# Seventy short unread products in a small planned stage: filling TensorE's waits in the first layer of a four-layer network

## The chip, the cores and the metric

The kernel runs on one core of a Trainium2 chip. The metric is the device time of one execution in microseconds (us), the median of a few executions; smaller is better. Beside the timed executions there is one profiled execution, whose span runs from its first to its last instruction.

A NeuronCore has five engines that work side by side and wait for each other on semaphores: TensorE (PE in the profile, its weight loads PEld), VectorE (DVE), ScalarE (ACT), GpSimd (POOL) and SyncE (SP), which only issues transfers here. Each engine takes its own instructions strictly in the order of its list. TensorE writes into PSUM, of which the kernel uses eight banks of 128 x 512 floats.

## The reference, cut to what matters

Four sub-layers follow each other on an input of 8 x 256 tokens with 128 features; after each comes a residual and a layer norm. The change lies in the first two.

```python
x = L0_attn_x                                       # 8 x 256 x 128
# first: a linear attention with a per-batch summary
Q = l2norm(x @ W_q.T); K = l2norm(x @ W_k.T); V = x @ W_v.T
x = layernorm(x + Q * (sum over tokens of K * V) / 128)
# second: a router and eight experts, two of them per token
h = layernorm(x @ Wr1 + br1) * ln_scale + ln_bias
logits = gelu(h) @ Wr2 + br2
p = softmax(logits); take the two largest, normalise them
x = layernorm(x + sum over the two experts of share * expert(x))
...
# then a convolution with four linear attentions, and a gated network
```

## The kernel before, in words

The 2048 tokens are worked as four blocks (`blk` 0 to 3) of 512 tokens, each block as four tiles of 128.

**The opening (lines 417 to 588).** `first_layer(blk)` describes one block's path through attention and router as a list of steps, each with an engine, a cost in ns, what it reads and writes, and the PSUM bank it needs. The steps of one block that matter below, by their names and lines:

- `project` (L440): four products per block, copied out by ACT (L443).
- `sums` (L475): four products that sum K * V over the tokens. They need `rk`, a reciprocal root from POOL (L334, L335), and `kv` from DVE (L467). `attend` (DVE, L486) reads the result, `residual` (L495) and `moments` (L343, L345) follow.
- `turned_s` (L503): four transposes; ACT copies them out (L509).
- `router` (L515): four products of 64 columns into the bank `pr`; `scaled` (DVE, L540) and another `moments` read them.
- `turned` (L559): two transposes of the normed router features `hn` (DVE, L550), then the gelu on ACT (L565).
- `choices` (L571): two products of 16 columns into `pl`, and DVE adds the bias into `logits` (L576).

`top_two` (L389 to L397) are thirteen DVE steps that pick two experts per token, once for blocks 0 and 1 and once for blocks 2 and 3. Their last step (L397) writes `taken`.

All these steps go into one object, `opening = Steps(...)` (L417). `Steps.order` is a list scheduler: it simulates the engines with the written costs, takes at each point the engine that can start first, and among the steps that this engine could start within `look` (50 ns) of that moment the one of highest rank plus bias. `Steps.trace` then emits the instructions in that order, under a manual schedule. So the costs in the code are used only to fix the order of each engine's list; on the chip an instruction starts when its data are there and its predecessor is out of the way.

**The counting stage (lines 595 to 689)** follows with a hand-written order. A DVE scan makes `upto` out of `taken` (L598). Two TensorE products (L603, L604) into the bank `pc` turn it into counts per expert. DVE works out of `pc` (L616 to L674) which slot each token gets; POOL finds the `owners` (L631 to L637), the expert of each of 23 work tiles. DVE then makes one-hot rows (L678) in four parts and TensorE multiplies 32 of them (L682), from which the list `source` comes.

In this stage TensorE also runs products that nobody reads: `busy(p)` multiplies the identity with 512 columns of a table (L593). Six stand behind L604 and four behind L682.

**Then the experts (lines 709 to 833):** SP loads an expert's weights per work tile as soon as `owners` is known, POOL gathers the rows by `source` (L749), and TensorE works in the order `turn` (L758), `widen` (L769), `narrow` (L782). The rest of the network, from line 835 on, has its own `Steps` object with its own list.

Of the kernel before, what the change touches and what calls it, by code (L numbers as in the profile page):

```python
# [220 lines left out]
def tile_network(ctx: ExitStack, tc: tile.TileContext, a: dict, out: bass.AP):  # L221
    nc = tc.nc
# [26 lines left out]
    def ps():  # L249
        return psp.tile([P, TB], F32, tag="ps", name="ps")  # L250
# [10 lines left out]
    ident = const.tile([P, P], F32, tag="ident", name="ident")  # L261
# [9 lines left out]
    def soon(shape, src, tag, pool=once):  # L271
        t = pool.tile(shape, F32, tag=tag, name=tag)
        nc.scalar.dma_start(out=t, in_=src)
        return t

    wqkv = soon([P, 3 * D], a["wqkv"], "wqkv")
# [42 lines left out]
    def tab(name):  # L319
        return tabs[:, TABS[name][0] : TABS[name][1]]  # L320
# [53 lines left out]
    def top_two(at):  # L374


        n = at.stop - at.start
        wide = [P, n, E]
        rev = mark("rev").unsqueeze(1).to_broadcast(wide)

        def spread(v):
            return v[:, at].unsqueeze(2).to_broadcast(wide)

        given, less, eq = logits[:, at, :], rest[:, at, :], key[:, at, :]
        steps = []
        for k, src in enumerate((given, less)):
            one = tops[:, k, at, :]
            steps += [
                lambda k=k, src=src: nc.vector.tensor_reduce(best[k][:, at], src, AX.X, ALU.max),  # L389
                lambda k=k, src=src: nc.vector.tensor_tensor(eq, src, spread(best[k]), ALU.is_equal),  # L390
                lambda: nc.vector.tensor_mul(eq, eq, rev),
                lambda: nc.vector.tensor_reduce(km[:, at], eq, AX.X, ALU.max),
                lambda one=one: nc.vector.tensor_tensor(one, eq, spread(km), ALU.is_equal),
            ]
            if k == 0:
                steps.append(lambda one=one: nc.vector.scalar_tensor_tensor(less, one, -1e30, given, ALU.mult, ALU.add))
        steps.append(lambda: nc.vector.tensor_add(  # L397
            taken[:, :, at].rearrange("p e i -> p i e"), tops[:, 0, at, :], tops[:, 1, at, :]))
        return steps
# [14 lines left out]
    nc.scalar.activation(once.tile([P, 1], F32, tag="warm", name="warm"), ones[:, 0:1], AF.Gelu_apprx_tanh)  # L414


    opening = Steps({"ps": [ps() for _ in range(8)]}, 50)  # L417

    def first_layer(blk):
        xT, x, w = xTs[blk], xs[blk], {}  # L420
# [3 lines left out]
        def do(engine, cost, run, reads="", writes="", later=0, new=""):  # L424
            def of(names):
                return [f"{n}.{blk}" for n in names.split()]

            opening.add(
                engine, cost, run, of(reads), of(writes) + of(new), {name: "ps" for name in of(new)}, bias=(0, -2464, -8107, -5328)[blk] - later
            )  # L430
# [127 lines left out]
                at = slice(i * P, (i + 1) * P)  # L558
                nc.tensor.transpose(T("pT")[:, at], w["hn"][:, at], ident)  # L559

        do("PE", 450, turned, "hn", new="pT")

        def gelu():
            w["hT"] = tmp()[:, : NT // 2 * P]
# [7 lines left out]
                    T("pl")[:, i * E : (i + 2) * E], lhsT=w["hT"][:, i // 2 * P : (i // 2 + 1) * P], rhs=wr2, start=True, stop=True  # L572
                )

        do("PE", 700, choices, "hT", new="pl")
        do("DVE", 190, lambda: nc.vector.tensor_add(  # L576
            logits[:, blk * NT : (blk + 1) * NT, :], T("pl")[:, : NT * E].rearrange("p (i e) -> p i e", i=NT), biases[:, R:].unsqueeze(1).to_broadcast([P, NT, E])
        ), "pl", "logits")

    for blk in range(NB):  # L580
        first_layer(blk)
    for blocks in ((0, 1), (2, 3)):
        for i, run in enumerate(top_two(slice(blocks[0] * NT, (blocks[-1] + 1) * NT))):
            opening.add(
                "DVE", 165 + 40 * len(blocks), run, [f"logits.{blk}" for blk in blocks] if i == 0 else [f"tops.{blocks[0]}"],
                [f"tops.{blocks[0]}"], bias=0 if blocks[-1] == NB - 1 else -50000,
            )
# [3 lines left out]
    def busy(p):  # L591

        return nc.tensor.matmul(p, lhsT=ident, rhs=tab("cos"), start=True, stop=True)  # L593


    with tc.manual_schedule():
# [2 lines left out]
            upto.rearrange("p e i -> p (e i)"), mark("later"), taken.rearrange("p e i -> p (e i)"), 0.0, ALU.mult, ALU.add  # L599
        )  # L600
        per_lane = upto[:, :, NTT - 1]
        pc = ps()
        nc.tensor.matmul(pc[:, 0:E], lhsT=ones, rhs=per_lane, start=True, stop=True)  # L603
        nc.tensor.matmul(pc[:, E : 2 * E], lhsT=mark("before"), rhs=per_lane, start=True, stop=True)  # L604

        idle = ps()
        for _ in range(6):
            busy(idle)

# [771 lines left out]
```

## Time and profile before

| what | us |
|---|---|
| median of 3 timed executions | 551.79 (551.04 to 553.66) |
| profiled execution, its own time | 549.38 |
| its span | 547.5 |
| opening, up to the last `logits` (L576) | ends at 42.97 |
| counting, up to the first gather (L749) | 42.97 to 59.15 |
| first TensorE instruction of the experts (L758) | 63.16 |
| the same stage's second `widen` (L769) | 69.55 |

TensorE is busy 508.9 us of the span (93%), DVE 283.9, ACT 221.0, POOL 212.1. These shares belong to the whole; the change touches only the first 59 us, where TensorE is not always the busiest.

How to read the views that come below. In the page's slices a digit is the busy share of one fortieth of the span, 13.7 us, in tenths, and `PEclk` is the clock that TensorE was granted, in tenths of full speed. A timeline row has the start, the length, the engine, the line, the operation, the tiles, the shape and the number of instructions merged into it, then in brackets the idle time before it and what ended it. A float32 product appears as two MATMUL rows, since it is done in two passes: the six `busy` of L593 are counted as twelve. A transpose is one pass. The chain of waits lists start, length, engine and line of the work that decided the end.

### The profile page before, as it was taken

To read this page: it belongs to the slowest core of one execution; us is meant where nothing else is said; L and a number is where in the kernel's file an instruction comes from. 1 tells how busy PE (TensorE), PEld (TensorE's weight loads), DVE (VectorE), ACT (ScalarE), POOL (GpSimd) and SP (SyncE) were. 2 spreads that over 40 slices of the span, in tenths; PEclk is the share of its full clock that TensorE was granted. 3 is DMA by queue.
4 is the path that set the end of the run, shared out by engine and by line. 5 is a ranking of instruction groups with operands and counts; after the bars stand their busy time and mean duration, and the time that the engine had idled before them with its cause. 6 is when DMAs were issued, how large, how long until landed. Compare 5 with 4: busy or idle time off the path is not lost.

```text
span 547.5 us, 7855 instructions
## 1 busy us (share of the span) xinstructions
PE 508.9 (93%) x2657; PEld 336.9 (62%) x2657; DVE 283.9 (52%) x955; ACT 221.0 (40%) x516; POOL 212.1 (39%) x310
## 2 busy tenths in 40 slices
PE   5877689999999999999999999989999999999992
PEld 3663478978999654458787886744444444444442
DVE  2887323433444385379899898687505530021212
ACT  3861223433444134237686868544224211322210
POOL 1971565666644321137666767361301000000001
PEclk9955989999999999999999999999999999999997
DMA  7951666665572320000000000000000000000010
GB/s 240 348 193 47 202 209 181 223 224 184 175 273 93 102 80 1 1 0 2 1 2 1 1 2 2 0 1 0 1 1 0 0 19 1 0 0 0 2 38 19
DMA packets 22889, 39.29 MB, mean 72 GB/s; under 512 B 3041, under 2 KB 16097, under 8 KB 22721
## 3 DMA queue, kind: packets, MB, share of 16 engines
q1 hardware_dynamic: 19088, 33.14, 18.4%
q0 software_dynamic: 2496, 5.12, 3.4%
q10 hardware_dynamic: 1264, 0.54, 0.4%
q8 instruction: 21, 0.34, 0.3%
q14 instruction: 20, 0.16, 0.1%
HBM read 34.13 MB, written 4.65 MB: 71 GB/s over the span
## 4 chain that ended last, share of the span: by engine, by line
PE 66%; DVE 12%; POOL 8%; issue 6%; DMA 4%; ACT 2%; SPq 1%; another core or an unknown queue 0%; POOLq 0%; DVEq 0%; ACTq 0%
PE ps L1256 20%; PE ps L769 10%; PE ps L1236 5%; PE ps L782 4%; POOL root L335 3%; PE ps L1277 3%; PE ps L997 2%; POOL ys L793 2%; PE ps L1017 2%; PE ps L1162 2%; DVE stats L878 2%; PE ps L1203 2%; PE ps L923 2%; PE ps L1192 2%; PE ps L1127 2%
## 5 line engine op out<-in xcount | busy, mean ns | idle before, releaser
L334 POOL TENSOR_SCALAR root<-mv 128x4 f32<-128x4 f32 (+1 forms) x46 | 12.5, 272 | 208.3 <-DVE mv L880 206.5
L769 PE MATMUL ps<-xT,hid 128*128 128x256 f32 (+1 forms) x368 | 75.2, 355 | 6.3 <-issue 5.9
L769 PEld LDWEIGHTS ps<-xT,hid 128*128 128x128 f32 x368 | 61.3, 194 | 15.3 <-issue 8.4
L775 DVE SCALAR_TENSOR_TENSOR gate<-ps,hid,gl 128x256 f32<-128x256 f32 (+1 forms) x92 | 38.6, 441 | 59.3 <-ACT gl L774 29.7
L774 ACT ACTIVATE gl<-ps,hid 128x256 f32<-128x256 f32 (+1 forms) x92 | 38.3, 445 | 50.4 <-PE ps L769 32.7
L1256 PE MATMUL ps<-t,gh 128*128 128x512 f32 x128 | 58.4, 592 | 0.0
L1256 PE MATMUL ps<-hid,gh 128*128 128x512 f32 x128 | 58.2, 592 | 0.0
L335 POOL TENSOR_TENSOR root<-root,minus_half 128x4 f32<-128x4 f32 (+1 forms) x54 | 55.1, 1020 | 4.5
L749 POOL DMA_INDIRECT xg<-x,source x39 | 37.8, 968 | 33.3 <-PE ps L769 11.0
L793 POOL DMA_INDIRECT ys<-y,dest x39 | 38.4, 984 | 23.6 <-DVE y L788 13.8
L1256 PEld LDWEIGHTS ps<-hid,gh 128*128 128x128 f32 x128 | 24.2, 190 | 29.7 <-issue 28.9
L1256 PEld LDWEIGHTS ps<-t,gh 128*128 128x128 f32 x128 | 24.0, 190 | 28.7 <-issue 28.7
L782 PE MATMUL ps<-hid,gate 128*128 128x128 f32 x312 | 38.8, 276 | 0.8 <-DVE gate L775 0.8
L782 PEld LDWEIGHTS ps<-hid,gate 128*128 128x128 f32 x312 | 37.9, 192 | 1.8 <-DVE gate L775 1.0
L1241 DVE SCALAR_TENSOR_TENSOR t<-t,ps 128x512 f32<-128x512 f32 x16 | 10.9, 681 | 51.2 <-ACT t L1239 51.2
L912 ACT ACTIVATE t<-t,shift,root 128x128 f32<-128x128 f32 x64 | 26.4, 482 | 10.8 <-POOL shift L892 10.8
L1236 PE MATMUL ps<-featT,g 128*128 128x512 f32 x64 | 30.2, 592 | 0.0
L1239 ACT ACTIVATE t<-ps,half 128x512 f32<-128x512 f32 x16 | 11.0, 687 | 41.3 <-PE ps L1236 41.3
L1113 POOL TENSOR_TENSOR t<-t,t 128x512 f32<-128x512 f32 x16 | 20.4, 1272 | 17.3 <-DVE t L1101 17.3
L1261 ACT ACTIVATE t<-ps,cols 128x512 f32<-128x512 f32 x16 | 11.0, 687 | 36.3 <-PE ps L1256 36.2
L923 PEld LDWEIGHTS ps<-ident,t 128*128 128x128 f32 x144 | 17.2, 141 | 11.6 <-issue 7.5
L878 DVE BATCH_NORM_STATS2 stats<-ps 128x6 f32<-128x128 f32 x48 | 10.7, 285 | 22.2 <-PE ps L923 22.1
(197 smaller groups left out, 940.9 us busy)
## 6 DMA issues: line engine op xcount, KB each, us to landing
hid<-in_experts_dram SPq DMA_DIRECT2D x23, 836.0 KB
got<-ys SPq DMA_DIRECT2D x6, 256.0 KB
counts<-in_counts_dram SPq DMA_DIRECT2D x1, 1032.0 KB
featT<-in_xT_dram SPq DMA_DIRECT2D x4, 256.0 KB
res<-in_x_dram SPq DMA_DIRECT2D x4, 256.0 KB
gh<-in_h1T_dram SPq DMA_DIRECT2D x1, 1024.0 KB
gh<-in_h2T_dram SPq DMA_DIRECT2D x1, 1024.0 KB
x<-res SPq DMA_DIRECT2D x4, 256.0 KB
```

Source lines behind the costliest of these rows:

```text
L335: nc.gpsimd.tensor_tensor(r, r, minus_half[:, :n], ALU.pow)
L749: landed[t] = nc.gpsimd.indirect_dma_start(out=rows_in[t][:, j, :], out_offset=None, in_=x1, in_offset=bass.IndirectOffsetOnAxis(ap=source ...
L769: keep(nc.tensor.matmul(p[:, half * m : (half + 1) * m], lhsT=part(t, "w1", half * F + c * P, P), rhs=xT, start=True, stop=True,))
L774: keep(nc.scalar.activation(gl, p[:, m : 2 * m], AF.Gelu_apprx_tanh, bias=part(t, "b1", FC + c, 1)))
L775: keep(nc.vector.scalar_tensor_tensor(g[:, c, :m], p[:, :m], part(t, "b1", c, 1), gl, ALU.add, ALU.mult))
L782: keep(nc.tensor.matmul(p[:, j * D : (j + 1) * D], lhsT=g[:, c, j * P : (j + 1) * P], rhs=part(t, "w2", c * D, D), start=(c == 0), stop=(c ...
L793: put = nc.gpsimd.indirect_dma_start(out=ys, out_offset=bass.IndirectOffsetOnAxis(ap=dest[:, u : u + 1], axis=0), in_=y[:, j, :], in_offse ...
L878: nc.vector.bn_stats(stats[:, i, :], by_tile(T(src))[:, at + i, :])
L912: nc.scalar.activation(by_tile(T(dst))[:, i, :], by_tile(T(src))[:, i, :], AF.Identity, bias=T(sh)[:, i : i + 1], scale=T(r)[:, i : i + 1],)
L923: nc.tensor.transpose(T(dst)[:, i * P : (i + 1) * P], T(src)[:, i * P : (i + 1) * P], ident)
L1236: do("PE", 853, lambda p=p, w=w, c=c: nc.tensor.matmul(T(f"{p}{c}"), lhsT=w[:, c * P : (c + 1) * P], rhs=T("xT"), start=True, stop=True), ...
L1256: do("PE", 853, lambda c=c, i=i, w=w, dst=dst, src=src: nc.tensor.matmul(T(f"p{dst}{c}"), lhsT=w[:, i, c * P : (c + 1) * P], rhs=chunk(src ...
```

## The change

Four things are edited.

1. The opening's planner gets seven PSUM banks instead of eight. The eighth, `idle`, is allocated there rather than in the counting stage.
2. Seventy new steps are added to the opening: a product of the identity with 128 columns of `wqkv` into `idle`, which nobody reads. Their written cost is 112 ns. Their bias of -1e6 makes them the last choice among what TensorE could start; the first needs block 1's `router` to have been issued (`behind=["pr.1"]`), and the others follow it through the name they share.
3. The written costs of `turned` go from 450 to 350 and of `choices` from 700 to 550.
4. In the counting stage six more `busy(idle)` are placed ahead of the two products into `pc`.

```diff
-    opening = Steps({"ps": [ps() for _ in range(8)]}, 50)
+    opening = Steps({"ps": [ps() for _ in range(7)]}, 50)
+    idle = ps()
...
-        do("PE", 450, turned, "hn", new="pT")
+        do("PE", 350, turned, "hn", new="pT")
...
-        do("PE", 700, choices, "hT", new="pl")
+        do("PE", 550, choices, "hT", new="pl")
...
     for blk in range(NB):
         first_layer(blk)
+
+    for i in range(70):
+        opening.add(
+            "PE", 112, lambda: nc.tensor.matmul(idle[:, :128], lhsT=ident, rhs=wqkv[:, :128], start=True, stop=True),
+            writes=["filler.3"], bias=-1e6, behind=["pr.1"] if i == 0 else (),
+        )
...
         per_lane = upto[:, :, NTT - 1]
+        for _ in range(6):
+            busy(idle)
         pc = ps()
         nc.tensor.matmul(pc[:, 0:E], lhsT=ones, rhs=per_lane, start=True, stop=True)
         nc.tensor.matmul(pc[:, E : 2 * E], lhsT=mark("before"), rhs=per_lane, start=True, stop=True)
...
-        idle = ps()
         for _ in range(6):
             busy(idle)
```

What the planner makes of it, in TensorE's list, from block 2's `turned_s` on (the number behind a name is the block, `f` is one of the seventy):

```
turned_s.2, 12 f, sums.3, 1 f, turned.0, router.2, 10 f, choices.0, turned_s.3,
10 f, router.3, turned.1, 8 f, choices.1, 13 f, turned.2, 9 f, turned.3, choices.2,
2 f, choices.3, 5 f, 6 busy, the two products into pc, 6 busy, 32 one-hot products, 4 busy
```

Before the change the same part reads:

```
turned_s.2, sums.3, turned.0, router.2, choices.0, turned_s.3, router.3, turned.1,
choices.1, turned.2, turned.3, choices.2, choices.3, the two products into pc,
6 busy, 32 one-hot products, 4 busy
```

Ahead of that, `sums.2` and `turned_s.1` change places, and some banks are assigned differently. On DVE two small steps on `half` and `both` (L841, L842), which belong to a later stage, move from between the `top_two` steps to just ahead of block 3's `attend`, and the first pair's `taken` (L397) moves from ahead of the last `logits` to the end, beside the second pair's. Block 2's `logits` goes one step earlier. The lists of ACT, POOL and SP are unchanged, and so is everything behind the counting stage.

## The prediction

> **What bounds the kernel now.** I read the page's slices first, then busy time in windows of 3.41 us, then the chain of waits from 38 us on, then TensorE's timeline.
>
> ```profile
> PE   5877689999999999999999999989999999999992
> PEclk9955989999999999999999999999999999999997
> ```
>
> TensorE fills the kernel from slice 6 on. The change works in slices 1 to 4, where the granted clock falls to half. The windows say when (columns: window, length, PE, PEld, DVE, ACT, POOL busy, clock, DMA share, GB/s):
>
> ```profile
> 25.15:28.56 3.41, 1.36 (x6) 0.84 (x7) 3.17 (x16) 2.72 (x13) 2.99 (x7) 1.00 1.05 387
> 28.56:31.97 3.41, 3.41 (x20) 3.41 (x19) 2.55 (x15) 2.17 (x7) 3.01 (x6) 0.54 1.08 360
> ...
> 49.04:52.45 3.41, 3.41 (x5) 1.35 (x4) 3.07 (x13) 0.00 (x0) 1.55 (x6) 0.50 0.01 2
> 52.45:55.87 3.42, 3.42 (x14) 1.60 (x13) 3.35 (x8) 0.00 (x0) 0.00 (x0) 0.95 0.77 264
> ```
>
> A window in which TensorE is busy 1.36 of 3.41 us is followed by half clock. A full one (28.56) doesn't undo that; one full of 512-column products (49.04) does. So the clock is low from about 28.8 to 52.6 us. What that costs is for the chain to say:
>
> ```profile
> 40.30 0.70 PE ps L559 x2
> ...
> 41.08 0.57 ACT tmp L565
> ...
> 41.70 1.05 PE ps L571 x4
> ...
> 42.78 0.20 DVE logits L576
> ...
> 46.13 0.44 DVE upto L598
> ...
> 46.70 0.56 PE ps L603 x2
> 47.27 0.43 PE ps L604 x2
> 47.69 7.83 PE ps L593 x12
> 55.53 2.65 PE ps L682 x32
> ```
>
> Up to 40 us the chain is DVE and POOL handing work to each other. TensorE enters with `turned` and `choices` of the last block, with the two products into `pc`, and with the six `busy`, which at half clock last until the one-hots are ready and a little longer (the first one-hot part leaves DVE at about 55.06, the first product starts at 55.36). Everything later hangs on this chain, so a shift here is a shift of the end.
>
> **What a filler costs.** No row shows one, but the same shape (128 x 128, float32) stands twice in the timeline at full clock:
>
> ```profile
> 14.84 1.05 PE L475 MATMUL ps<-tmp,root 128*128 128x128 f32 x8
> 15.73 2.10 PE L440 MATMUL ps<-wqkv,featT 128*128 128x384 f32 x6
> ...
> 90.69 1.95 PE L782 MATMUL ps<-hid,gate 128*128 128x128 f32 x16
> 92.48 0.38 PE L758 MATMUL ps<-ident,xg 128*128 128x128 f32 x2
> ```
>
> From start to start: 0.89/8 = 0.111 and 1.79/16 = 0.112 us a pass. Four `sums` are eight passes, so a filler is two: **0.224 us**, twice the 112 ns that the planner books. At half clock it would be 0.45.
>
> [...]
>
> **The change, part by part.** All at full clock (see below for that).
>
> *Fillers before the last `choices`.* TensorE leaves block 2's `turned_s` at about 26.74 (its last transpose waits for `residual`, which ends at 26.5; this is unchanged). From there the list is without a gap, since every filler is ready:
>
> - 65 fillers x 0.224 = 14.56
> - `sums.3`, 8 passes x 0.111 = 0.89; `turned_s.3`, 4 x 0.108 = 0.43
> - two `router`, 16 passes x 0.104 (20.29 to 21.12 for eight) = 1.66
> - four `turned`, 8 transposes x 0.107 (29.64 to 30.07 for two at half clock, halved) = 0.86
> - four `choices`, 16 passes x 0.102 (31.66 to 32.48 for four, halved) = 1.64
>
> Sum 20.04, so the last `choices` ends at 46.8; before it ended at 42.74. Its inputs are there: `choices.0` ends near 34.2 rather than 32.6, and as DVE takes `logits.0` ahead of block 3's `moments`, that chain slips by about 1 us, `router.3` (37.7 against 36.2) delays `scaled.3`, and `hn.3` comes near 41.6; `turned.3` stands in TensorE's list at 45.3. So TensorE, not DVE, sets the pace. Loss: **+4.05**.
>
> *Tail.* 5 fillers (1.12) and 6 `busy` (12 passes x 0.43, the pitch of L593's passes at full clock = 5.16) stand ahead of `pc`: its first product starts at 46.8 + 6.28 = 53.06, before 46.70. DVE's `upto` would be ready at 46.8 + 3.83 (42.74 to 46.57) + 0.27 for the moved `taken` = 50.9, so the six `busy` add 2.2 of their own. The two products are then 4 passes and a drain, 0.6 instead of 1.03 (46.70 to 47.73, where DVE's L616 starts). `pc` is read at 53.66 against 47.73: **+5.93**.
>
> *After `pc`.* DVE needs 7.33 us to the first one-hot part; the second six `busy` now take 5.2 and end before it. The 0.2 to 0.3 us by which TensorE was late at 55.36 go: **-0.2**. `owners` (POOL) and the weight loads behind them move by the whole 5.93, `source` and the gathers by 5.73. The rest of the lists is equal, so I carry +5.8.
>
> *Seven banks and the changed order* cost nothing. `sums.2` now goes first, at about 22.75 when `kv.2` is ready; `turned_s.1` and its copy on ACT come 1.1 us later, and so do ACT's copies for block 3, done near 26.4. DVE reads them only at 27.50 (L467), and `scaled.1` at 28.07. Without that cover: up to 1.1. One `project` waits 0.2 for a bank that ACT empties at 19.78. `half` and `both` (0.25 us on DVE) fall into the wait for `sums.3`; they need `cols`, whose transfer was issued at 9.61, and the chain shows `wq`, issued at 11.18, landed at 19.33. If `cols` were later than 30, DVE would stand still, at most until 38.95, where it is read today. I take 0.
>
> [...]
>
> **Sum.** 549.38 (profiled) + 5.8 = 555.2. The median of the runs shown lies 2.4 above the profiled one, so I forecast 551.79 + 5.8 = **557.6**.
>
> **Rivals.**
>
> 1. *TensorE is the pace and the clock holds* (557.6), chance 0.62. For it: 128-column streams (L782, L769) run at 1.00 from 100 to 200 us. Its own range is 555.8 to 559.4: 10% on the filler's price is 1.6, and the throttled stretch at 69.5 to 73 us (L769 x16 takes 5.41 there, 3.62 at full clock) may fall differently, up to 1.8 either way.
> 2. *The clock fails in places*, 0.24, about 560. Fillers reach only the second half of the window from 25.15, so 28.8 to 32.2 may be at half clock: +1.7. And TensorE now idles from 58.8 to 61.1, followed by one-hot products of 39 columns; if that window is judged low, half of them (+1.2) and the four `busy` behind them run slowly, and these then stand in front of the first `turn`: up to +1.9 together. Against it: 59.28 to 62.69 had TensorE busy 2.36 of 3.41 today and kept the clock.
> 3. *Not slower: a filler costs what the planner books*, 0.08. At one pass (0.112) the list ends at 39.5, DVE sets the last `choices` at about 41.9 (0.9 earlier by the clock), and only the six `busy` ahead of `pc` bind: 41.9 + 0.56 + 5.16 = 47.6, +0.3 in the end: 552.1. In general the sum is 70 x price - 9.95, so it turns at **0.142 us** a filler. For it speaks only the written cost; against it, eight MATMUL rows for four `sums`.
> 4. *The fillers don't lift the clock*, 0.04: TensorE's part doubles, 65 x 0.45 + 11 = 40 us from 26.74 on, then 13.5; `pc` comes 33 us late: 585. For it: the full window at 28.56 that stayed slow. Against it: that one was made of transposes, 64 and 16 columns in good part.
> 5. *Faster*, 0.02: rival 3 and the slow stretch at 69.5 gone (-1.8): 550.3.
>
> **How the numbers follow.** A difference of 0.5%, 2.8 us, is about what a measurement can tell from none. Rivals 1, 2 and 4 lie beyond it on the slow side (0.90, less a little for the low end of 1: 0.89); rival 3 within (0.08); 0.03 for faster. The range takes 1 and 2 with their ends, 554.6 to 561.0, and leaves out 3, 4 and 5, about 0.15.
>
> **What would show it.** In the profile after: fillers as 140 MATMUL rows at 0.112 us start to start; clock 1.00 from 28 to 58 us; the last `choices` ending near 46.8; no TensorE idle from 27 to 58; L616 near 53.7 with PE as its releaser, and the first gather near 64.9. I am wrong if fillers stand 0.11 us apart each, if DVE's `upto` comes after the six `busy`, or if a stretch at half clock falls among the fillers.

## The result, and the profile after

The changed kernel takes 560.17 us (median of 6 executions, 557.59 to 561.2) against 551.7 before, measured beside it (550.77 to 553.66): a ratio of 1.0138, 95% interval 1.0114 to 1.0162. Measured once more later, beside the experiments below, it takes 545.76 us against 539.35: 1.0117 (1.0102 to 1.0131). The two intervals overlap.

One name in what stands above has to be put right first. The block that is worked third is block 3, and block 2 comes last; in the lists of the change and in the prediction the numbers 2 and 3 are exchanged. No time depends on it. In the changed kernel, lines from 418 on have numbers one higher than before, those behind the fillers (L586) seven to nine higher: `sums` is L476, `choices` L572, `busy` L600, `pc` L612 and L613, the one-hot products L690.

The clock did what the change wants of it. From the page of the changed kernel, TensorE's clock in 40 slices of 14.0 us:

```profile
PE   5999868998999999999999999989999999999992
...
PEclk9999778999999999999999999999999999999997
```

Slices 2 and 3 (counted from 0), at half clock before, are at full clock, and the windows in which it fell before (columns as before) are full ones now:

```profile
25.15:28.56 3.41, 3.41 (x31) 3.17 (x30) 3.41 (x19) 3.41 (x15) 3.08 (x5) 1.00 1.04 387
28.56:31.97 3.41, 3.41 (x33) 3.41 (x33) 2.89 (x17) 2.07 (x6) 2.92 (x7) 1.00 1.07 365
```

Later it is lower than before: slices 4 to 6 have 7, 7 and 8 where they had 9, 8 and 9. There the clock is at half from 61.4 to 68.2 us, from 75.0 to 81.9 and from 92.1 to 95.5; before, it was so only from 69.9 to 73.3 in this part.

But the chain of waits (start, length, engine, line, instructions) has changed hands. Before, DVE and POOL made up the opening; now it reads

```profile
34.08 2.23 PE ps L586 x20
...
39.51 3.00 PE ps L586 x26
...
46.23 1.21 PE ps L586 x10
47.44 5.15 PE ps L600 x12
```

TensorE, without a gap, and its largest pieces are products that nobody reads: 26 passes of fillers take 3.00 us. The timeline of TensorE shows what follows behind the six `busy` (columns as before; the number behind x counts passes):

```profile
52.43 0.28 PE L612 MATMUL ps<-upto,ones 128*128 128x8 f32 x2
...
60.40 2.84 PE L690 MATMUL ps<-oh_hi,hid 128*128 128x39 f16 x32 [2.21 <-DVE hid L686]
63.06 6.21 PE L600 MATMUL ps<-tabs,ident 128*128 128x512 f32 x8
69.11 0.27 PE L766 MATMUL ps<-ident,xg 128*128 128x128 f32 x1
```

and DVE's says who waits for it:

```profile
33.70 0.19 DVE L577 TENSOR_TENSOR logits<-ps,biases 128x32 f32<-128x32 f32 x1 [1.04 <-PE ps L572]
...
45.35 0.19 DVE L577 TENSOR_TENSOR logits<-ps,biases 128x32 f32<-128x32 f32 x1 [2.87 <-PE ps L572]
...
49.83 0.42 DVE L605 TENSOR_TENSOR_SCAN upto<-marks,taken 128x128 f32<-128x128 f32 x1
52.97 0.29 DVE L624 TENSOR_TENSOR over<-marks,ps 128x128 f32<-128x128 f32 x1 [2.72 <-PE ps L613]
```

At 33.70 and 45.35 DVE stands idle for `choices` (L572), 1.04 and 2.87 us; at 52.97 it waits 2.72 us for the products into `pc`, since `upto` (L605) was ready at 50.25 and the six `busy` ahead of `pc` ran until 52.4. So both of TensorE's added pieces have DVE waiting behind them. Then the one-hot products wait 2.21 us for DVE, and the four `busy` behind them need 6.21 us instead of 3.66: the clock had fallen to half at 61.4.

### The profile page after: what moved, and what is told of

It is laid out like the page before. It is cut to its first block, busy times and chain, and to the rows that moved or that the text cites. A ratio compares the mean times of both kernels' runs of the same rounds, so it can differ in the third digit from the quotient of the medians.

```text
span 559.1 us, 8159 instructions
## 1 busy us (share of the span) xinstructions
PE 524.1 (94%) x2809; PEld 350.4 (63%) x2809; DVE 284.3 (51%) x955; ACT 220.7 (39%) x516; POOL 211.7 (38%) x310
## 4 chain that ended last, share of the span: by engine, by line
PE 71%; DVE 11%; POOL 7%; issue 6%; ACT 2%; DMA 2%; another core or an unknown queue 0%; POOLq 0%; ACTq 0%; DVEq 0%; SPq 0%
PE ps L1264 20%; PE ps L777 10%; PE ps L1244 5%; PE ps L790 4%; PE ps L586 3%; PE ps L1285 2%; PE ps L1005 2%; POOL ys L801 2%; PE ps L1025 2%; DVE stats L886 2%; PE ps L441 2%; PE ps L1170 2%; PE ps L1211 2%; PE ps L600 2%; PE ps L1200 2%
## 5 line engine op out<-in xcount | busy, mean ns | idle before, releaser
L777 PE MATMUL ps<-xT,hid 128*128 128x256 f32 (+1 forms) x368 | 76.4, 361 | 9.5 <-issue 6.6
L777 PEld LDWEIGHTS ps<-xT,hid 128*128 128x128 f32 x368 | 62.7, 198 | 18.6 <-issue 8.2
L1264 PEld LDWEIGHTS ps<-hid,gh 128*128 128x128 f32 x128 | 24.2, 190 | 29.7 <-issue 28.9
L600 PE MATMUL ps<-tabs,ident 128*128 128x512 f32 x56 | 27.4, 644 | 0.0
```

Source lines behind the costliest of these rows:

```text
L777: keep(nc.tensor.matmul(p[:, half * m : (half + 1) * m], lhsT=part(t, "w1", half * F + c * P, P), rhs=xT, start=True, stop=True,))
L1264: do("PE", 853, lambda c=c, i=i, w=w, dst=dst, src=src: nc.tensor.matmul(T(f"p{dst}{c}"), lhsT=w[:, i, c * P : (c + 1) * P], rhs=chunk(src ...
```

## The experiments

All but the last were timed in 5 rounds beside the kernel before, in two groups: the first four runs on a chip that the record calls 0, the last four on one that it calls 6. The kernel before takes 539.5 and 539.35 us there. For the first measurement (551.7 us) the record names no chip. The runs are told in the order in which they ran. For comparing places in the profile I take three marks: the start of the third `turned_s` (it moves by up to 1.7 us between executions of these runs), the start of `over`, DVE's first reader of `pc`, and TensorE's first `turn` of the experts. In the table, which is worked out from the timelines, the second and third columns are differences of these marks. The last column compares each run with the kernel before in its own group.

| run | third `turned_s` to `over` | `over` to first `turn` | ratio to before (95%) |
|---|---|---|---|
| before, profiled again | 21.92 | 15.26 | 1 |
| the change, measured again | 27.74 | 15.29 | 1.0117 (1.0102 to 1.0131) |
| no six ahead of `pc` | 25.78 | 15.24 | 1.0074 (1.0056 to 1.0092) |
| six alone | 25.33 | 15.29 | 1.0050 (1.0031 to 1.0068) |
| one-pass fillers | 22.12 | 15.71 | 1.0002 (0.9990 to 1.0014) |
| change with bridge | 27.75 | 15.26 | 1.0123 (1.0099 to 1.0146) |
| one pass, trimmed | 20.81 | 15.24 | 0.9977 (0.9961 to 0.9993) |
| priced, trimmed | 20.78 | 15.28 | 0.9984 (0.9970 to 0.9999) |

The rows of its first two marks, for the kernel before and then for the change:

```profile
25.25 1.11 PE L503 MATMUL ps<-ident,tmp 128*128 128x128 f32 x4 [0.94 <-DVE tmp L495]
47.17 0.29 DVE L616 TENSOR_TENSOR over<-marks,ps 128x128 f32<-128x128 f32 x1 [1.18 <-PE ps L604]
...
25.77 0.86 PE L504 MATMUL ps<-ident,tmp 128*128 128x128 f32 x4
53.51 0.29 DVE L624 TENSOR_TENSOR over<-marks,ps 128x128 f32<-128x128 f32 x1 [2.72 <-PE ps L613]
```

**Without the six `busy` ahead of `pc`.**

```diff
-        for _ in range(6):
-            busy(idle)
         pc = ps()
```

> The change without the six busy ahead of the two products into pc; the 70 fillers stay. Theory (TensorE's list is the pace, and each part adds what its passes take): the fillers keep their part of the loss, the six busy lose theirs, the 2.3 to 2.7 us by which DVE's over waits for pc in the changed kernel (L624 idle 2.72). over starts near 50.9 instead of 52.97, time about 2.1 below the changed kernel: 558. Rival (the loss beyond 53 us, in the experts' stage, is what matters and the six busy are covered by it): within 0.5 us of the changed kernel, 560.

It took 543.91 us. TensorE's first product into `pc` now waits for DVE, not DVE for it:

```profile
51.49 0.36 PE L610 MATMUL ps<-upto,ones 128*128 128x8 f32 x2 [2.95 <-DVE upto L605]
```

`over` comes 1.96 us sooner after the mark than with the change (25.78 against 27.74), and the ratio is 0.0043 below that of the change, 2.3 us of 539. The expected absolute times were those of the first measurement and don't compare, here and below; the difference of 2.1 does. So the six cost about 2 us, and 3.9 of the 5.8 remain with the fillers.

**The six alone.** One filler is kept, behind the last `choices`, to hold the six in their place.

```diff
-    for i in range(70):
+    for i in range(1):
...
-            writes=["filler.3"], bias=-1e6, behind=["pr.1"] if i == 0 else (),
+            writes=["filler.3"], bias=-1e6, behind=["pl.2", "pl.3"],
```

> The six busy ahead of pc alone: one filler instead of 70, placed behind the last choices so that the six stay where they are. Theory: the last choices ends at 42.7 as before the change, but the six now run at half clock for most of their length (12 passes at 0.86 until a full window has lifted it near 49, then 0.43), so pc is read near 52 instead of 47.73 and the time is about 4 us above before: 555.8. Rival (what six busy cost is paid back by the clock being up earlier, behind pc): within 0.5 us of before, 551.7.

542.19 us, a ratio of 1.0050: a loss of 2.7 us, less than the 4 expected, but clear of the noise.

```profile
42.18 7.46 PE L600 MATMUL ps<-tabs,ident 128*128 128x512 f32 x12
```

The twelve passes take 7.46 us; at full clock 5.32. At 0.85 and 0.43 us a pass, the spacing of the passes of L593 at half and at full clock in the first profile of before, that is some five slow passes, where I had reckoned with seven or eight. The rival, that a clock raised early pays them back, falls. The run also shows that the two parts don't simply add: the six cost 3.4 us between the marks when they stand alone and run slowly in part, 2.0 behind the fillers. And it has the seven banks and the changed order without the fillers: its last `choices` ends 17.1 us behind the first mark, against 16.9 before. So these two cost next to nothing.

**Fillers of one pass.** The same 70 places, the same lists, but a transpose in each.

```diff
-            "PE", 112, lambda: nc.tensor.matmul(idle[:, :128], lhsT=ident, rhs=wqkv[:, :128], start=True, stop=True),
+            "PE", 112, lambda: nc.tensor.transpose(idle[:, :128], wqkv[:, :128], ident),
```

> The 70 fillers as transposes of the same 128 columns: one pass of about 0.108 us each, which is what the planner books; the order of every list is that of the changed kernel. Theory (the price of two passes is the loss): TensorE's list no longer sets the pace, the last choices ends near 42, pc is read near 48.2, and the time is 552 to 554, the upper end if the clock still falls in the gap before the one-hots. Rival A (the order of the list, the extra instructions or the bank are the loss): 560, as the changed kernel. Rival B (transposes don't hold the clock up, so each is 0.21): last choices near 46 or later, 558 or more.

539.34 us, a ratio of 1.0002, just below what the theory gave (552 to 554 on 551.7, so 1.0005 to 1.004). Both rivals, with 558 us or more, fall. This is the run that decides. TensorE's timeline:

```profile
26.20 1.47 PE L586 MATMUL ps<-ident,wqkv 128*128 128x128 f32 x12
...
41.93 5.32 PE L600 MATMUL ps<-tabs,ident 128*128 128x512 f32 x12
```

Twelve fillers take 1.47 us instead of 2.84, and TensorE reaches the six `busy` at 41.9 rather than 47.8. The clock was 1.00 all the way to 55.2 us here too, so in this run transposes in the gaps, together with the products around them, kept it up. What is left of the loss in the opening is due to the six, for which DVE still waits 2.10 us:

```profile
47.63 0.29 DVE L624 TENSOR_TENSOR over<-marks,ps 128x128 f32<-128x128 f32 x1 [2.10 <-PE ps L613]
```

Number of steps, order and bank are those of the change, so these are not the loss; the time of the second pass is. Behind `over` this run takes 0.4 us longer than the others:

```profile
57.71 5.80 PE L600 MATMUL ps<-tabs,ident 128*128 128x512 f32 x8
63.34 0.27 PE L766 MATMUL ps<-ident,xg 128*128 128x128 f32 x1
```

The clock fell to half from 55.2 to 62.0 us, the four `busy` behind the one-hots ended late, and the first `turn` follows them without a wait for its rows, 15.71 us behind `over`.

**A bridge to the one-hots.**

```diff
-        for _ in range(6):
+        for _ in range(8):
             busy(idle)
```

(the `busy` behind `pc`)

> The changed kernel with eight instead of six busy behind pc, which fill 1.7 of the 2.2 us that TensorE waits for the one-hots (L690). Theory (the part of the loss beyond the opening is the clock, which falls near 62 us because of that gap): clock stays 1.00 from 60 to 69, the four busy behind the one-hots take 3.6 instead of 6.2, the first turn is at 68.1 instead of 69.11, time 1 to 3 us below the changed kernel: 557 to 559. Rival (the experts' first tiles wait for weights and rows, not for TensorE): the first turn comes earlier but the second widen (77.60) stays, and the time is within 0.5 us of 560.

545.66 us, which can't be told from the change (1.0123 against 1.0117), as the rival said. The clock theory was half right: the gap ahead of L690 shrank and the four `busy` ran at full clock,

```profile
60.75 2.82 PE L690 MATMUL ps<-oh_hi,hid 128*128 128x39 f16 x32 [0.48 <-DVE hid L686]
63.39 3.66 PE L600 MATMUL ps<-tabs,ident 128*128 128x512 f32 x8
68.60 0.30 PE L766 MATMUL ps<-ident,xg 128*128 128x128 f32 x1 [1.55 <-DMA xg<-x,source]
```

but the first `turn` is released by the rows' arrival, not by TensorE, and comes 15.26 us after `over` with the bridge and 15.29 without. The slow stretch of the change, 3.4 us in the profile of the next run, costs nothing; the one of 6.8 us in the one-pass run did cost 0.4.

**The change again, with its timeline.**

> The changed kernel once more, beside the runs that undo a part of it. Theory (the loss is made before the experts and adds up from the parts): 1.0123 (the run with the two bridging busy) plus about 0.5 to 1 us for the slow four busy that stand ahead of the first turn: ratio 1.013 to 1.015, on a chip that needs 539.5 before the change 546.5 to 547.5. Rival (the stall of 5.6 us ahead of the second widen in the first profile of the changed kernel belongs to it): second widen again some 8 us after the first one, and ratio 1.016 or more.

```profile
60.92 2.82 PE L690 MATMUL ps<-oh_hi,hid 128*128 128x39 f16 x32 [2.20 <-DVE hid L686]
63.56 4.84 PE L600 MATMUL ps<-tabs,ident 128*128 128x512 f32 x8
68.80 0.30 PE L766 MATMUL ps<-ident,xg 128*128 128x128 f32 x1 [0.40 <-DMA xg<-x,source]
...
72.23 3.72 PE L777 MATMUL ps<-xT,hid 128*128 128x256 f32 x16 [0.50 <-ACT xT L768]
```

1.0117, a little under the 1.013 to 1.015 expected: the loss is made ahead of the experts, as the theory has it, but the 0.5 to 1 us that I added for the slow four `busy` is not there. They take 4.84 us, and TensorE still waits 0.40 us for the rows behind them. The second `widen` (72.23) follows 3.4 us behind the first `turn`, as in every one of these eight runs; the rival is out. In the first profile of the changed kernel it was 8.49 us, and in the first one of before 6.39. So that longer wait doesn't come from the change alone.

**One pass, trimmed.** Transposes, three `busy` ahead of `pc` (2.6 us of cover for DVE's 3.6), eight behind.

```diff
-            "PE", 112, lambda: nc.tensor.matmul(idle[:, :128], lhsT=ident, rhs=wqkv[:, :128], start=True, stop=True),
+            "PE", 112, lambda: nc.tensor.transpose(idle[:, :128], wqkv[:, :128], ident),
...
-        for _ in range(6):
+        for _ in range(3):
             busy(idle)
         pc = ps()
...
-        for _ in range(6):
+        for _ in range(8):
             busy(idle)
```

> Transposes as fillers (one pass), three instead of six busy ahead of pc, eight instead of six behind it. Theory: three busy (2.6 us) fit under top_two and the scan (3.6), so pc is read at about 46.3 rather than 47.73; the two added ones keep the clock up over the one-hots, so the four busy behind them end before the first rows come, and the first turn is near 61.6 instead of 63.2: 1.5 us below before, ratio 0.996 to 0.998. Rival (TensorE's clock in the opening is worth nothing since DVE and POOL set its pace): ratio 0.999 to 1.001.

537.86 us, a ratio of 0.9977 (0.9961 to 0.9993): a little faster than before, and so than both kernels.

```profile
44.83 0.36 PE L612 MATMUL ps<-upto,ones 128*128 128x8 f32 x2 [1.00 <-DVE upto L605]
52.86 2.83 PE L690 MATMUL ps<-oh_hi,hid 128*128 128x39 f16 x32 [0.48 <-DVE hid L686]
```

`pc` now waits 1.00 us for DVE. `over` is 1.11 us nearer to the mark than before. In these 20.8 us the clock is 1.00 throughout and nothing unread holds up `pc`: so much is full clock worth in the opening. From `over` on nothing is won; the first `turn` waits for the rows as before. The ratio lies in the range expected, but the part of the reason that spoke of the two added `busy` fails.

**Booked at its price.** The products of the change, 33 of them, at 224 ns; the last stands behind the last `choices`; three and eight `busy`.

```diff
-    for i in range(70):
+    for i in range(33):
...
-            "PE", 112, lambda: ...
+            "PE", 224, lambda: ...
```

> The products of the change, but 33 of them, booked at 224 ns, which is what two passes take; three busy ahead of pc and eight behind. Theory: the list has 33 x 0.224 = 7.4 us of fillers, and TensorE no longer sets the pace at the end; each filler can still hold up a real step by up to 0.2 us, so the last choices ends near 42.3: pc read near 46.8, ratio 0.997 to 0.999. Rival (unread float32 products cost whatever their number): about half the loss of the 70, ratio 1.003 or more.

538.04 us, 0.9984 (0.9970 to 0.9999). Between the marks 20.78 us, the same as with the transposes. So 33 float32 fillers, booked at what they take, do no harm. Their number and their price were changed together, and three `busy` were taken away; which of these matters most, this run alone doesn't tell (70 booked at 224 ns, or 33 at 112, were not tried).

**Before, profiled again.**

> The kernel before, for a profile of it from the same chip as the other runs. Both theories: 539.5 if it is the chip of the first four runs, pc read near 47.7 and the first turn near 63.2 as in its first profile. What it tells apart is the experts' stage: if TensorE waits 3.5 us ahead of the second widen here too, that wait belongs to the kernel; if not, to the chip or the execution.

```profile
46.14 0.56 PE L603 MATMUL ps<-upto,ones 128*128 128x8 f32 x2 [3.96 <-DVE upto L598]
46.99 7.71 PE L593 MATMUL ps<-tabs,ident 128*128 128x512 f32 x12
54.59 2.82 PE L682 MATMUL ps<-oh_hi,hid 128*128 128x39 f16 x32
...
65.86 3.72 PE L769 MATMUL ps<-xT,hid 128*128 128x256 f32 x16 [0.50 <-ACT xT L760]
```

539.31 us (one execution). The opening is like that of the first profile (`over` at 47.17 against 47.73), though the clock came back in between: it is at half from 27.8 to 31.2 us and from 34.6 to 51.7, 20.5 us in all, where the first profile has 23.9 us in one piece. In both, TensorE was busy throughout the first 3.4 us at half clock; full clock followed here and not there. So the prediction's reading that such a stretch doesn't undo half clock holds for one profile only, and what decides stays open. Between the marks it makes no difference: 21.92 us here, 21.94 in the first profile.

The second `widen` is 3.4 us behind the first `turn`. From it to the start of the last `narrow` product it takes 105.6 us here, 112.2 in the first profile of before, 115.9 in the first of the changed kernel. So the first measurement's executions spend 7 to 10 us more in that stage, and the two kernels' profiles differ there by 3.7 us, with the same instructions. Part of this is the clock: in that stretch of the first profiles it is at half for 3.4 us before and for 7.7 us after, and in this one and the change's second one not at all. Sixteen passes of `widen` take 5.41 us in the first profile of before, with 3.4 us at half clock, and 3.62 at full clock. What makes TensorE wait there in the first measurement stays open, and so does whether it is the chip; no run here tells it.

## Why the prediction was right

*The sum.* It was +5.8 us. Between the marks in the later runs it is 27.74 - 21.92 = 5.82, and the medians there differ by 6.4. The first measurement, 8.5, is larger. Between its marks it has the same 5.80; but its two profiles differ by 0.7 us more up to the first `turn`, by 2.1 from there to the second `widen`, and by 3.7 in the rest of the experts. The sum had none of this, and the later runs don't repeat it. So the mechanism and its size in the opening are confirmed. But rival 1's own range ends at 559.4; the range as a whole reaches 561.0 by rival 2's allowance for the clock, and only a part of what exceeds 557.6 came that way. That 560.17 falls within it is in part luck.

*The price of a filler.* 0.224 us was expected; 24 passes from 25.93 to 28.61 in the changed kernel are 2.68, or 0.223 for two. They are 140 rows more, as said. At about 0.11 us a filler, in the one-pass run, TensorE is waiting for DVE again ahead of the last `turned` (0.58 us); at 0.223 the chain up to `over` consists of TensorE almost alone.

*The last `choices`.* Forecast to end at 46.8, with `turned_s` at 25.79; it ended at 46.23, with `turned_s` at 25.23. Reckoned from the mark that is 21.0 in both.

*The six `busy`.* 2.2 us of their own were forecast; taking them away brings 1.96.

*After `pc`.* Here 0.2 us were to come back. From `over` to the first `turn` it is 15.29 us against 15.26: nothing came back. The slow `busy` of the kernel before ended at 54.7 in its second profile, and the one-hots began at 54.59, so there was nearly no lateness to remove. With it left out the forecast would have been 6.0.

*The clock.* In the first profile of the changed kernel it held (1.00 in every window from 25.15 to 59.28 us), as rival 1 said, and then fell, at 61.4 us, where rival 2 put the danger, behind the gap before the one-hots. All four profiles with a gap of 2.2 us there (the changed kernel twice, the six alone, one pass) show half clock within 3 us behind it, for 3.4 us twice and for 6.8 us twice; of the six with 0.5 us or none (the kernel before twice, the run without the six, the bridge and the two trimmed ones) none does. Ahead of `pc` it was alike: behind the wait of 2.95 us in the run without the six the clock is at half from 53.2 to 56.6 us, behind those of 1.00 and 1.28 us in the trimmed ones it stays full (1.00 up to 73.2). What rival 2 made of that, up to 1.9 us, came in part where the low stretch was long: 0.4 us in the one-pass run, and in the first profile of the changed kernel, where the slow `busy` ended after the rows had come and the first `turn` was 4.88 us behind the gather's start instead of 4.01, 0.9 us. Where it was 3.4 us long, the rows arrived late enough to hide it (the bridge saves nothing).

*What a higher clock gives.* On the chain before stand 0.70 + 1.05 + 0.99 us of slow products (its rows at 40.30, 41.70, 46.70 and 47.27): 1.4 us when halved, an estimate from these rows. The two trimmed kernels hold full clock through the opening (1.00 in all windows from 22.0 to 52.7 us) and gain 1.1 us between the marks, and 1.2 and 0.9 us in all by their ratios. The estimate is near this. The 23.9 us at half clock in the first profile of before are no measure of it: from 28.9 up to 40.30 and from 42.78 to 46.70 the chain has DVE and POOL, not TensorE.

*Rival 3, the price.* At one pass each 552.1 was forecast, +0.3. The one-pass run is +0.2 between the marks, and 1.0002 in time. That supports the sum at both prices; the turning point of 0.142 us itself was not tried.

## What to carry to other kernels

A list that a planner writes is only as good as its costs: here seventy steps booked at half their price (0.112 us for 0.224) filled gaps that weren't there, and what stood behind them in TensorE's list came late, the products into `pc` among it: in the run without the six `busy`, `over` came 3.9 us later behind the mark than before. Before filling an engine's waits, read the price of the filler's shape from the trace, counting passes, and let what is added fit under the work that the engine waits for. And reckon a clock at half speed by the slow instructions on the chain of waits: here about 1.1 us were won between the marks at full clock, where TensorE had stood at half clock for 20.5 us.

## What the hardware showed that I had not expected

- With float32 transposes in the gaps the granted clock stays at 1.00 up to 55.2 us, where without fillers it fell at 27.8 and 28.9 us. With the products of the change it stays at 1.00 up to 61.4 us, at twice the time (2.84 us for twelve against 1.47).
- A wait of TensorE of 2.2 us, followed by products of 39 columns, was followed by half clock in four profiles of four, for 3.4 or 6.8 us. A wait of 0.5 us in the same place was not, in four of four.
- The kernel before took 551.7 us in one measurement and 539.4 in another, with openings that agree within 0.6 us.
